# A graph layer's opening: index loads behind the first rows of x, and ACT's order fixed in the tables

## The chip, the cores and the metric

The kernel runs on one core of one Trainium2 chip. The metric is device time in microseconds (us) of one execution, lower being better. The engines are named as in the profile: PE (matrix products and transposes), PEld (PE's weight loads), DVE (vector), ACT (scalar), POOL (GpSimd) and SP (which here only issues DMAs).

## The reference

One layer of a graph network on 6,250 nodes with 128 features and 100,000 edges, sorted by destination, followed by a residual and a layer norm:

```python
msg_in = concatenate([x[src], x[dst]], axis=-1)
h = relu(msg_in @ Wm1 + bm1)
h = relu(h @ Wm2 + bm2)
messages = h @ Wm3 + bm3
agg = segment_sum(messages, dst) / clip(count(dst), 1)
upd = relu(concatenate([x, agg], axis=-1) @ Wn1 + bn1) @ Wn2 + bn2
out = layernorm(x + (x + upd))
```

All data are float32, the indices int32.

## The kernel before

**Three stages.** The product with `Wm1` is taken per node and not per edge: A = x @ Wm1[:128] and B = x @ Wm1[128:] are written to two tables in DRAM, `atab` (float32) and `btab` (each row as three bfloat16 terms whose sum is the float32 row). The main loop then takes the edges in 196 groups of 512, in four pieces of 128: it gathers rows of A by `src` (POOL's indirect DMA, L412), loads a window of rows of B for each piece (SP, L418), spreads them by one-hot matrices made from the destinations, and runs the second product, and sums by destination into `acc` in SBUF. A last stage updates the nodes. The change lies in the tables, but for one copy that it puts into the main loop.

**Loads at the start.** SP loads x into `x_sb` (first tiles 0 and 1, then 2 and 3, then block 1, then two blocks at a time; a block is four tiles of 128 nodes), then `w2`, `w3` and `wu1`. ACT loads `w1` and then `dst_i`, the destinations; POOL loads `src_i`, the sources, and five bias vectors. From `dst_i`, DVE works out each piece's first node: `dst_f` (L190) and its reductions down to `diag` (L274).

**The tables.** There are 13 blocks of nodes (`BLOCKS`; the last has one tile). Round i of the loop at L336 stands in PE's list, which is the order written here since PE is under a manual schedule:

- `turn(4 * i + 4)`: the next block's four transposes into a bank of `pp` (3 buffers), which ACT copies to `xT` (L267). Block 0 is turned ahead of the loop.
- `a_table` for tiles 4i and 4i + 2: `products` of two tiles into a bank of `pb` (5 buffers), copied by ACT (L241) into one of 6 buffers of `brow`, and written by SP to `atab` (L242).
- at i = 6 `starts()`: three products against `diag` whose results (`spread`) DVE copies out (L283 to L296); at i = 7 and 8 `columns`, which transposes the indices into `srcT` and `dloc` (L304, L306).
- `b_table` for tiles 4(i - 3) and on: ACT casts the product (first term, L249), DVE takes the rest (L250, after which the bank is free), POOL casts the rest (second term, L252; ACT at L254 for the last four blocks), DVE takes the third term (L255), SP writes the row to `btab` (L256).
- from i = 12 on, `x_part` for blocks 0 to 2 (`X_BESIDE`): two products of a whole block with `wu1` (L316), each taken out with the bias by ACT (L318) or DVE (L320). Blocks 3 to 8 (`X_BEHIND`) follow the loop.

After the loop `destinations` is called three times: a one-element copy by DVE (L357) that makes the load wait for `srcT`, and two DMAs on ACT's queue of destinations, spread over partitions (`db`, L361). From there to group 6 of the main loop ACT and DVE too are under a manual schedule. POOL clears `acc` in 24 pieces (L376). `pb3` (L381) is a small product whose result DVE adds (L382).

**Order.** Outside the manual schedules a scheduler sets each engine's order from priorities and its own estimates, so a line's place in the source isn't its place in the engine's list; `tc.high_priority()` puts the first loads ahead. Each engine works through its list in order, and a wait holds what stands behind it.

**The copy of the destinations.** `dpad` is a copy of `dst` in DRAM with filler at its end, read only by a loop at L611 that handles windows too wide for one pass and does not run for these inputs. Its two DMAs (L539, L540) stand in the source at group 16 of the main loop; the scheduler had put the first of them behind `wu1`'s load, at 14 us.

Of the kernel before, what the change touches and what calls it, by code (L numbers as in the profile page):

```python
# [11 lines left out]
I32 = mybir.dt.int32  # L12
# [3 lines left out]
ENG = mybir.EngineType  # L16
# [3 lines left out]
P = 128  # L20
# [7 lines left out]
def kernel(  # L28
# [122 lines left out]
    with tc.tile_pool(name="prep", bufs=1) as prep, tc.tile_pool(  # L151
# [8 lines left out]
        nc.vector.memset(dst_i[tail:, :], NONE)  # L160
        with tc.high_priority():
            nc.scalar.dma_start(w1, wm1.rearrange("(k p) h -> p k h", p=P))
            load_rows(nc.scalar, dst_i, dst)
            load_rows(nc.gpsimd, src_i, src)
            with nc.allow_non_contiguous_dma(reason="a bias, one value a partition"):
                nc.gpsimd.dma_start(b1, bm1.rearrange("(c p) -> p c", p=P))
                nc.gpsimd.dma_start(b2, bm2.rearrange("(c p) -> p c", p=P))
                nc.gpsimd.dma_start(b3, bm3.rearrange("(c p) -> p c", p=P))
                nc.gpsimd.dma_start(bu1, bn1.rearrange("(c p) -> p c", p=P))
            nc.gpsimd.dma_start(nb2[:, 0, :], bm2.rearrange("(o h) -> o h", o=1).to_broadcast([P, H]))  # L170

            xb = x[:NTF * P, :].rearrange("(b p i) d -> p b i d", p=P, i=4)
            for i0 in (0, 2):
                nc.sync.dma_start(x_sb[:, i0:i0 + 2, :], xb[:, 0, i0:i0 + 2])
            t = 4
            for n in (4, 8, 8, 8, 8, 8):
                n = min(n, NTF - t)
                nc.sync.dma_start(x_sb[:, t:t + n, :].rearrange("p (b i) d -> p b i d", i=4),
                                  xb[:, t // 4:(t + n) // 4])
                t += n  # L180
            assert t == NTF
            nc.sync.dma_start(x_sb[:N - NTF * P, NTF, :], x[NTF * P:, :])
        nc.sync.dma_start(w2, wm2.rearrange("(k p) h -> p k h", p=P))
        nc.sync.dma_start(w3, wm3.rearrange("(k p) h -> p k h", p=P))
        nc.sync.dma_start(wu1, wn1.rearrange("(k p) h -> p k h", p=P))
# [31 lines left out]

        order = ExitStack()
        order.enter_context(tc.manual_schedule(engines={ENG.PE}))

# [15 lines left out]
        def a_table(t0):  # L236
            m = min(2, NT - t0)
            pbt = products(t0, m, 0)
            bt = brow.tile([P, 2 * 3 * H], BF16, name="bt")
            rows = bt[:, :2 * 2 * H].bitcast(F32).rearrange("p (t h) -> p t h", t=2)  # L240
            nc.scalar.copy(rows[:, :m], pbt[:, :m])  # L241
            nc.sync.dma_start(atab[t0 * P:(t0 + m) * P, :].rearrange("(t p) h -> p t h", p=P), rows[:, :m])  # L242

        def b_table(t0):
            m = min(2, NT - t0)
            pbt = products(t0, m, 1)
            bt = brow.tile([P, 2 * 3 * H], BF16, name="bt").rearrange("p (t c h) -> p t c h", t=2, c=3)
            rest = brow.tile([P, 2, H], F32, name="rest", bufs=2)
            nc.scalar.copy(bt[:, :m, 0], pbt[:, :m])  # L249
            nc.vector.tensor_sub(rest[:, :m], pbt[:, :m], bt[:, :m, 0])  # L250
            if t0 < 4 * LATE:
                nc.gpsimd.tensor_copy(bt[:, :m, 1], rest[:, :m])  # L252
            else:
                nc.scalar.copy(bt[:, :m, 1], rest[:, :m])  # L254
            nc.vector.tensor_sub(bt[:, :m, 2], rest[:, :m], bt[:, :m, 1])  # L255
            nc.sync.dma_start(btab[t0 * P:(t0 + m) * P].rearrange("(t p) c h -> p t c h", p=P), bt[:, :m])  # L256

        def turn(t0):
            m = min(4, NT - t0)
            pt = pp.tile([P, 4, P], F32, name="pt", tag="pp")  # L260
            for i in range(m):
                n = min(P, N - (t0 + i) * P)
                nc.tensor.transpose(pt[:, i, :n], x_sb[:n, t0 + i, :], ident[:n, :n])
            w = min(m * P, N - t0 * P)
            block = xT[:, t0 * P:t0 * P + w]
            if m == 4:
                nc.scalar.copy(block.rearrange("p (n i) -> p i n", i=4), pt)  # L267
            else:
                nc.scalar.copy(block, pt[:, 0, :w])
# [53 lines left out]
        def whole(steps):  # L323
            for _ in steps:
                pass
# [9 lines left out]
        turn(0)  # L335
        for i in range(BLOCKS + BEHIND):  # L336
            if i + 1 < BLOCKS:
                turn(4 * i + 4)
            if i < BLOCKS:
                for t0 in range(4 * i, min(4 * i + 4, NT), 2):  # L340
                    a_table(t0)
            if i == INDICES:
                starts()
            if i - INDICES in (1, 2):
                columns(i - INDICES - 1)
            if i >= BEHIND:
                for t0 in range(4 * (i - BEHIND), min(4 * (i - BEHIND) + 4, NT), 2):
                    b_table(t0)
            if BLOCKS - 1 <= i < BLOCKS - 1 + len(X_BESIDE):
                whole(x_part(X_BESIDE[i - BLOCKS + 1], bank_pb, (nc.scalar, nc.scalar)))  # L350

        def destinations(g, ng, dst_row):

            db = ld.tile([P, 2, 2 * P], I32, name="db", bufs=3)
# [7 lines left out]
            return [db[:, k, :] for k in range(ng)]  # L362

        dst_row = dst.rearrange("(o e) -> o e", o=1)
        early = [destinations(2 * k, 2, dst_row) for k in range(3)]

        turns = ExitStack()
        turns.enter_context(tc.manual_schedule(engines={ENG.DVE, ENG.Activation}))
        for b in X_BEHIND:
            whole(x_part(b, bank_pb, (nc.scalar, nc.vector)))  # L370

# [23 lines left out]
    with edge, tc.tile_pool(name="wk", bufs=2) as wk, tc.tile_pool(  # L395
# [136 lines left out]
        for i in range(NG + ahead + 1):  # L532
            if i == 6:
                turns.close()
            if i == 16:
                late_loads()
                none = wk.tile([16, (NG * GE - E) // 16], I32, name="none", bufs=1)
                nc.vector.memset(none, NONE)
                nc.sync.dma_start(dpad[:E].rearrange("(p e) -> p e", p=16), dst.rearrange("(p e) -> p e", p=16))  # L539
                nc.sync.dma_start(dpad[E:].rearrange("(p e) -> p e", p=16), none)  # L540
            for step, after in enumerate((20, 24, 27)):
                if i >= after and (i - after) % 8 == 0 and (i - after) // 8 < len(pieces):
                    double((i - after) // 8, step)
# [252 lines left out]
```

## Time and profile before

| | |
|---|---|
| median of 5 runs | 1449.77 us (1447.51 to 1451.92) |
| the profiled execution | 1450.33 us, span 1448.6 us |
| mean granted clock of PE | 0.987 |
| busy share of the span | PE 86%, PEld 63%, DVE 46%, ACT 31%, POOL 56% |
| bytes read and written in DRAM | 168.92 MB and 22.88 MB, 132 GB/s over the span |
| first transposes, first product of the tables | 3.86 us, 9.81 us |
| first gather, last line of `btab` issued | 66.79 us, 78.5 us |
| first product of the main loop | 90.77 us |

In a line of a timeline the columns are the start in us, the time in us from there to the end of the last of the merged instructions, the engine, the line of the kernel, the operation with its output and inputs, shapes, and the number of instructions; in brackets stands how long the engine was idle before it and what ended that. An engine with a "q" is its queue, where a DMA is issued. In a table by stages each stretch has busy us and instructions of PE, PEld, DVE, ACT and POOL, then the granted clock of PE (1.00 is full), the mean busy share of the 16 DMA engines, and GB/s.

### The profile page before, as it was taken

The numbers are of one execution on the slowest core, as the hardware profiler recorded it, in microseconds if no ns is written. First come the engines' busy times: TensorE is split into PE (matmuls) and PEld (weight loads), VectorE is DVE, ScalarE is ACT, GpSimd is POOL, SyncE is SP. The second block draws the span as 40 slices with busy tenths as digits, with TensorE's granted clock in tenths as the row PEclk, the third lists the DMA queues.
The fourth block names the chain that finished last, engine by engine and source line by source line (L and its number), as shares of the span: only waits on it lengthen the run. The fifth ranks groups of instructions, "written<-read, shape, count | busy, mean of one in ns | idle before, by whom it ended". The sixth has DMA issues, their size and how long they took to land. (4 is left out here: it accounts for less than half of the span.)

```text
span 1448.6 us, 32804 instructions
## 1 busy us (share of the span) xinstructions
PE 1249.0 (86%) x11196; PEld 918.3 (63%) x11197; DVE 661.1 (46%) x2083; ACT 453.1 (31%) x1160; POOL 805.7 (56%) x859
## 2 busy tenths in 40 slices
PE   7978888888888888888888888898888888888997
PEld 6746666666666666666666666666666666666656
DVE  5733444444443434444444444444443444434487
ACT  5632323232322323232222323232232322323246
POOL 7356565555656556555556556555555556555031
PEclk9989999999999999999999999999999999999999
DMA  8855565555444444444444444444444444443043
GB/s 277 301 154 145 147 162 143 159 139 149 125 122 124 117 128 122 124 114 124 125 121 127 116 127 125 121 114 124 125 124 127 116 125 126 123 122 108 14 146 113
DMA packets 173672, 193.66 MB, mean 134 GB/s; under 512 B 30844, under 2 KB 145486, under 8 KB 173488
## 3 DMA queue, kind: packets, MB, share of 16 engines
q0 software_dynamic: 37984, 103.35, 26.4%
q1 hardware_dynamic: 106956, 61.93, 14.5%
q10 hardware_dynamic: 28564, 26.27, 6.6%
q8 instruction: 90, 1.47, 0.4%
q14 instruction: 78, 0.64, 0.1%
HBM read 168.92 MB, written 22.88 MB: 132 GB/s over the span
## 5 line engine op out<-in xcount | busy, mean ns | idle before, releaser
L412 POOL DMA_INDIRECT ag<-atab,srcT x784 | 753.6, 961 | 524.4 <-PE ph L455 310.6
L469 PE MATMUL ph<-w,h 128*128 128x256 f32 x3128 | 736.5, 389 | 1.4 <-issue 1.4
L469 PEld LDWEIGHTS ph<-w,h 128*128 128x128 f32 x3128 | 583.7, 192 | 158.7 <-issue 61.9
L460 ACT ACTIVATE h<-ph,b 128x256 f32<-128x256 f32 x782 | 306.3, 474 | 914.1 <-PE ph L455 824.5
L471 DVE TENSOR_TENSOR h<-ph,nb 128x512 f32<-128x512 f32 x391 | 269.7, 692 | 688.6 <-PE ph L449 294.1
L455 PE MATMUL ph<-oht,bw 64*128 64x128 bf16 x1564 | 126.8, 217 | 159.8 <-issue 151.2
L455 PEld LDWEIGHTS <-bw 64*128 64x128 bf16 x1564 | 67.4, 95 | 201.4 <-issue 174.3
L494 DVE TENSOR_TENSOR acc<-acc,pt 128x63 f32 x782 | 172.9, 221 | 30.6 <-PE pt L489 2.3
L449 PE MATMUL ph<-ident,ag 64*128 64x64 f32 x3128 | 133.0, 223 | 13.6 <-DVE b L382 7.4
L478 PE MATMUL pg<-h,oh 128*32 128x257 f32 x1564 | 129.8, 397 | 3.2 <-PE ph L455 2.3
L449 PEld LDWEIGHTS ph<-ident,ag 64*128 64x128 f32 x3128 | 114.3, 139 | 13.2 <-DVE b L382 7.5
L433 DVE TENSOR_SCALAR oht<-db,pbase 128x128 bf16<-128x128 int32 x392 | 104.3, 296 | 5.5 <-remote 5.1
L489 PEld LDWEIGHTS pt<-ident,part 64*128 64x128 f32 x1173 | 51.0, 136 | 65.6 <-issue 64.5
L481 ACT COPY part<-pg 128x257 f32<-128x257 f32 x196 | 76.6, 391 | 4.0 <-PE pg L478 4.0
L489 PE MATMUL pt<-ident,part 64*128 64x64 f32 x1173 | 77.7, 238 | 0.0
L436 DVE TENSOR_TENSOR oh<-iota_n,dloc 128x128 f32<-128x128 f32 x196 | 55.7, 284 | 2.8 <-PE pg L478 1.9
L677 POOL TENSOR_TENSOR agg<-total,rc 128x512 f32<-128x512 f32 (+2 forms) x15 | 16.0, 1069 | 70.1 <-DVE total L674 63.3
L232 PE MATMUL pbt<-w,xT 128*128 128x256 f32 x196 | 49.0, 396 | 2.0 <-ACT bt L241 1.4
L478 PEld LDWEIGHTS pg<-h,oh 128*32 128x32 f32 x1564 | 32.1, 108 | 27.2 <-issue 6.1
L232 PEld LDWEIGHTS pbt<-w,xT 128*128 128x128 f32 x196 | 37.0, 198 | 10.5 <-ACT bt L241 2.6
L252 POOL CAST bt<-rest 128x512 bf16<-128x512 f32 x18 | 12.2, 686 | 26.9 <-DVE rest L250 17.9
L700 PEld LDWEIGHTS pot<-wu,u 128*128 128x128 f32 (+1 forms) x196 | 24.0, 191 | 5.1 <-issue 4.5
(110 smaller groups left out, 418.9 us busy)
## 6 DMA issues: line engine op xcount, KB each, us to landing
bw<-btab SPq DMA_DIRECT2D x782, 32.0 KB
db<-in_dst_dram ACTq DMA_DIRECT2D x194, 128.0 KB
ag<-atab,srcT POOLq DMA_INDIRECT x784
btab<-bt SPq DMA_DIRECT2D x24, 384.0 KB
atab<-bt SPq DMA_DIRECT2D x24, 256.0 KB
xd<-in_x_dram SPq DMA_DIRECT2D x12, 256.0 KB
x2tab<-xd SPq DMA_DIRECT2D x12, 256.0 KB
x_sb<-in_x_dram SPq DMA_DIRECT2D x5, 512.0 KB
```

What stands on the lines that cost most here:

```text
L232: nc.tensor.matmul(pbt[:, a, :], xT[:, (t0 + a) * P:(t0 + a + 1) * P], w1[:, k, :], start=True, stop=True)
L412: nc.gpsimd.indirect_dma_start(out=ag[:, j, :], out_offset=None, in_=atab[:, :], in_offset=bass.IndirectOffsetOnAxis(ap=idx[:, j:j + 1], a ...
L433: nc.vector.tensor_scalar(oht[:n, k, :], db[:n, k * P:(k + 1) * P], pb_cols[:n, k:k + 1], None, op0=ALU.is_equal)
L449: nc.tensor.matmul(phs[h][:, c, u * NQ:(u + 1) * NQ], ag[halves[h], u, c * P:(c + 1) * P], ident[halves[h], halves[h]], is_transpose=True, ...
L455: nc.tensor.matmul(phs[h][:, c, k * P:(k + 1) * P], bw[halves[h], k, c * P:(c + 1) * P], oht[halves[h], k, :], start=False, stop=True, ski ...
L460: nc.scalar.activation(h1[:, c, h * 2 * P:(h + 1) * 2 * P], phs[h][:, c, :], AF.Relu, bias=b1[:, c:c + 1])
L469: nc.tensor.matmul(ph2[:, a, :], h1[:, c, (j0 + a) * P:(j0 + a + 1) * P], w2[:, c, :], start=(c == 0), stop=(c == HC - 1))
L471: nc.vector.tensor_tensor(h2[:, j0:j0 + 2, :H], ph2, nb2.to_broadcast([P, 2, H]), op=ALU.max)
L478: nc.tensor.matmul(pg[j * WN:(j + 1) * WN, :], oh[:, j, :], h2[:, j, :], start=True, stop=True, skip_group_check=True)
L481: nc.scalar.copy(part[:n, :], pg[:n, :])
L489: nc.tensor.matmul(pt[:, c, :], rows, ident[halves[h], halves[h]], is_transpose=True, start=True, stop=True, skip_group_check=True)
L494: nc.vector.tensor_add(window, window, pts[j // 2][:, :, k:k + WB])
```

## The change

- `dst_i` and `src_i` are loaded from POOL's queue, without high priority, as are the biases; ACT's queue starts with `w1` alone.
- In round 0 the first `a_table` stands ahead of the second block's transposes; the other rounds are as before.
- The last four blocks' b rows get their later terms (`b_terms`) one table later.
- `destinations` is called in rounds 10, 11 and 12, behind the b tables, and not after the loop.
- The x parts of blocks 0 to 2 are taken out by ACT and DVE, and not by ACT alone.
- ACT is under a manual schedule from the start of the tables: its order is that of the source.
- `dpad` gets its filler first, over an end that is 16 elements longer, so that the copy of `dst` has to wait for it and stays at group 16.

```diff
         with tc.high_priority():
             nc.scalar.dma_start(w1, wm1.rearrange("(k p) h -> p k h", p=P))
-            load_rows(nc.scalar, dst_i, dst)
-            load_rows(nc.gpsimd, src_i, src)
...
...
             nc.sync.dma_start(x_sb[:N - NTF * P, NTF, :], x[NTF * P:, :])
+
+        load_rows(nc.gpsimd, dst_i, dst)
+        load_rows(nc.gpsimd, src_i, src)
...
...
         order.enter_context(tc.manual_schedule(engines={ENG.PE}))
+        turns = ExitStack()
+        turns.enter_context(tc.manual_schedule(engines={ENG.Activation}))
...
+        unfinished = []
         def b_table(t0):
...
             nc.vector.tensor_sub(rest[:, :m], pbt[:, :m], bt[:, :m, 0])
+            unfinished.append((t0, m, bt, rest))
+            if len(unfinished) > 1 or t0 < 4 * LATE:
+                b_terms()
+
+        def b_terms():
+            t0, m, bt, rest = unfinished.pop(0)
             if t0 < 4 * LATE:
                 nc.gpsimd.tensor_copy(bt[:, :m, 1], rest[:, :m])
...
+        early = []
         turn(0)
         for i in range(BLOCKS + BEHIND):
-            if i + 1 < BLOCKS:
-                turn(4 * i + 4)
-            if i < BLOCKS:
-                for t0 in range(4 * i, min(4 * i + 4, NT), 2):
-                    a_table(t0)
+            tiles = range(4 * i, min(4 * i + 4, NT), 2) if i < BLOCKS else []
+            for n, t0 in enumerate(tiles):
+                if n == (i == 0) and i + 1 < BLOCKS:
+                    turn(4 * i + 4)
+                a_table(t0)
...
+            if BLOCKS - 3 <= i < BLOCKS:
+                early.append(destinations(2 * len(early), 2, dst_row))
             if BLOCKS - 1 <= i < BLOCKS - 1 + len(X_BESIDE):
-                whole(x_part(X_BESIDE[i - BLOCKS + 1], bank_pb, (nc.scalar, nc.scalar)))
+                whole(x_part(X_BESIDE[i - BLOCKS + 1], bank_pb, (nc.scalar, nc.vector)))
+        b_terms()
-        early = [destinations(2 * k, 2, dst_row) for k in range(3)]
-        turns = ExitStack()
-        turns.enter_context(tc.manual_schedule(engines={ENG.DVE, ENG.Activation}))
+        turns.enter_context(tc.manual_schedule(engines={ENG.DVE}))
...
             if i == 16:
                 late_loads()
-                none = wk.tile([16, (NG * GE - E) // 16], I32, name="none", bufs=1)
+                none = wk.tile([16, (NG * GE - E) // 16 + 1], I32, name="none", bufs=1)
                 nc.vector.memset(none, NONE)
+                nc.sync.dma_start(dpad[E - 16:].rearrange("(p e) -> p e", p=16), none)
                 nc.sync.dma_start(dpad[:E].rearrange("(p e) -> p e", p=16), dst.rearrange("(p e) -> p e", p=16))
-                nc.sync.dma_start(dpad[E:].rearrange("(p e) -> p e", p=16), none)
```

By the built programs, POOL's 24 memsets of `acc`, which stood almost all ahead of its first cast, now stand as 6 ahead of the first cast, 1 behind it, 4 behind the second, and 5 and 8 behind the next two pairs; and DVE's share of an early x part stands ahead of the rests of the two b tables written before it.

More of the change, by code (lines that the diff above doesn't have):

```diff
@@ L162 @@
             nc.scalar.dma_start(w1, wm1.rearrange("(k p) h -> p k h", p=P))
-            load_rows(nc.scalar, dst_i, dst)
-            load_rows(nc.gpsimd, src_i, src)
[L165 to L170, printed above, removed]
             xb = x[:NTF * P, :].rearrange("(b p i) d -> p b i d", p=P, i=4)
@@ L182 @@
             nc.sync.dma_start(x_sb[:N - NTF * P, NTF, :], x[NTF * P:, :])
+        load_rows(nc.gpsimd, dst_i, dst)
+        load_rows(nc.gpsimd, src_i, src)
+        with nc.allow_non_contiguous_dma(reason="a bias, one value a partition"):
+            nc.gpsimd.dma_start(b1, bm1.rearrange("(c p) -> p c", p=P))
+            nc.gpsimd.dma_start(b2, bm2.rearrange("(c p) -> p c", p=P))
+            nc.gpsimd.dma_start(b3, bm3.rearrange("(c p) -> p c", p=P))
+            nc.gpsimd.dma_start(bu1, bn1.rearrange("(c p) -> p c", p=P))
+        nc.gpsimd.dma_start(nb2[:, 0, :], bm2.rearrange("(o h) -> o h", o=1).to_broadcast([P, H]))
         nc.sync.dma_start(w2, wm2.rearrange("(k p) h -> p k h", p=P))
@@ L333 @@
         assert sorted(X_BESIDE + X_BEHIND + X_FIRST + X_END) == list(range(BLOCKS))
-        turn(0)
-        for i in range(BLOCKS + BEHIND):
-            if i + 1 < BLOCKS:
-                turn(4 * i + 4)
-            if i < BLOCKS:
-                for t0 in range(4 * i, min(4 * i + 4, NT), 2):
-                    a_table(t0)
[L342 to L349, printed above, removed]
-                whole(x_part(X_BESIDE[i - BLOCKS + 1], bank_pb, (nc.scalar, nc.scalar)))
         def destinations(g, ng, dst_row):
@@ L364 @@
         dst_row = dst.rearrange("(o e) -> o e", o=1)
-        early = [destinations(2 * k, 2, dst_row) for k in range(3)]
-        turns = ExitStack()
-        turns.enter_context(tc.manual_schedule(engines={ENG.DVE, ENG.Activation}))
+        early = []
+        turn(0)
+        for i in range(BLOCKS + BEHIND):
+            tiles = range(4 * i, min(4 * i + 4, NT), 2) if i < BLOCKS else []
[3 more added lines that the diff above has]
+                a_table(t0)
+            if i == INDICES:
+                starts()
+            if i - INDICES in (1, 2):
+                columns(i - INDICES - 1)
+            if i >= BEHIND:
+                for t0 in range(4 * (i - BEHIND), min(4 * (i - BEHIND) + 4, NT), 2):
+                    b_table(t0)
+            if BLOCKS - 3 <= i < BLOCKS:
+                early.append(destinations(2 * len(early), 2, dst_row))
+            if BLOCKS - 1 <= i < BLOCKS - 1 + len(X_BESIDE):
+                whole(x_part(X_BESIDE[i - BLOCKS + 1], bank_pb, (nc.scalar, nc.vector)))
+        b_terms()
+        turns.enter_context(tc.manual_schedule(engines={ENG.DVE}))
         for b in X_BEHIND:
```

## The prediction

> **What bounds the kernel now.** I read the busy time by stages first, to see where the edited code runs and what is full there; then the timelines of PE, ACT, DVE, POOL and SP up to 95 us, because every edit but one lies before the first group of edges. The main loop, from 91 us on, executes the same groups after the change as before, so the question is when it starts.
>
> Stages (us of the stretch, busy us of each engine, clock, DMA share):
>
> ```profile
> 14.00:24.00 10.00, 9.78 (x50) 8.22 (x48) 7.10 (x17) 6.38 (x10) 9.02 (x13) 1.00 1.03 359
> 36.00:50.00 14.00, 13.47 (x79) 11.61 (x78) 13.79 (x29) 8.50 (x14) 3.31 (x5) 1.00 0.76 264
> 50.00:63.00 13.00, 11.67 (x51) 8.40 (x49) 8.02 (x13) 8.45 (x16) 4.14 (x7) 1.00 0.98 344
> 63.00:83.00 20.00, 19.67 (x57) 10.43 (x57) 13.41 (x21) 14.14 (x26) 13.76 (x15) 1.00 0.85 283
> 83.00:91.00 8.00, 0.58 (x9) 0.50 (x9) 1.87 (x10) 0.69 (x1) 3.42 (x4) 0.73 0.33 98
> ```
>
> The first number after the stretch is PE's. PE carries the tables (90 to 98% busy from 14 to 83 us), DVE is as full from 36 to 50, DMA is full at 14 to 24 and 50 to 63, and from 83 to 91 everything is idle.
>
> PE's timeline at the two ends of the tables:
>
> ```profile
> 8.90 1.11 PE L263 MATMUL pt<-ident,x_sb 128*128 128x128 f32 x4 [2.02 <-DMA x_sb<-in_x_dram]
> 9.81 3.62 PE L232 MATMUL pbt<-w,xT 128*128 128x256 f32 x8
> 14.07 2.34 PE L232 MATMUL pbt<-w,xT 128*128 128x256 f32 x8
> ...
> 36.72 0.60 PE L263 MATMUL pt<-ident,x_sb 128*128 128x128 f32 x4
> ...
> 60.52 2.42 PE L232 MATMUL pbt<-w,xT 128*128 128x256 f32 x10 [0.55 <-ACT bt L241]
> 72.47 10.55 PE L316 MATMUL pxu<-xT,wu 128*128 128x512 f32 x24
> 90.77 1.12 PE L449 MATMUL ph<-ident,ag 64*128 64x64 f32 x16 [7.42 <-DVE b L382]
> ```
>
> I write a0, a2, ... and b0, b2, ... for the products of `a_table` and `b_table`. a0 starts at 9.81, behind the second block's transposes, which wait for x; a4 starts at 14.07; b38, the last b ahead of the x parts, ends at 62.94; the last x part ends at 83.02; the first group starts at 90.77.
>
> POOL, ACT, and SP's loads of the first groups:
>
> ```profile
> 7.23 15.79 POOL L376 MEMSET acc<- 128x784 f32 x21
> 66.79 1.05 POOL L412 DMA_INDIRECT ag<-atab,srcT  x1 [2.58 <-DMA atab<-bt]
> 46.71 1.42 ACTq L361 DMA_DIRECT2D db<-in_dst_dram  x2
> 48.24 1.07 ACT L249 CAST bt<-pbt 128x512 bf16<-128x512 f32 x2 [3.93 <-PE pbt L232]
> 64.78 14.07 SPq L256 DMA_DIRECT2D btab<-bt  x9
> 82.81 33.65 SPq L418 DMA_DIRECT2D bw<-btab  x32
> ```
>
> The chain that opens the main loop is the last line of `btab`: issued at 78.51, landed at 81.94, first `bw` issued at 82.81, the fourth at 89.83, first L455 at 91.67. Beside it runs the x parts' chain: L320 at 89.90, L382 at 90.57, which frees the bank for L449. Both end within 2 us of each other, so a gain must move both.
>
> **The change part by part.**
>
> *First rows.* Without `dst_i` on ACT's queue and `src_i` on POOL's at 1.3 us, x's first three pieces and `w1` (0.77 MB) are alone. At 0.3 MB a us (0.24 up to 14 us, 0.36 from there to 24), from the first packet at 2.7 us, and with the 0.7 us from bytes to landing, block 1 is there at about 6, not 8.86. The first transposes then end at about 4.9, ACT's copy (1.07) at 6.0, a0 takes 1.8 (half of the 3.62, at that same rate), the moved transposes 1.1, a2 1.8 and the next transposes about 0.7: a4 at about 11.1 instead of 14.07. **Lead 3.0**; 3.4 with the faster clock that in this trace comes 5 us after a0.
>
> *Indices.* `dst_i` now follows POOL's iotas (about 2.6 us instead of 1.29) and is POOL's DMA. `src_i` by that queue took 7.3 us from issue to landing, `dst_i` by ACT's 5.4. So `dst_f` starts at about 10.5 (before 10.24), and `diag`, which ended at 21.46, is needed at 33.3. Cost 0; cover 12 us. The Trainium skill, "SBUF — State Buffer", in its warning on DVE blocking a POOL DMA, speaks against the move: POOL cannot write descriptors while DVE holds the shared port, and its example grows from 0.6 to 3.1 us. Here POOL's three `src_i` issues took 0.75, 0.53 and 0.49 beside DVE's two 0.91 memsets, so the trace does not show it; by the rule the three issues of `dst_i` would be 7.5 us later, still inside that cover, and the sum the same.
>
> *`dpad` held back.* Its 390 KB sat between the weights and the first `atab` row in SP's queue: a0 landed at 21.34, 0.64 behind it, while `dpad` took 0.95. a12's copy reuses a0's buffer, so it moves from 23.81 to about 20.5 (in the old order it also stood behind a block copy). At group 16 the copy costs SP one issue (0.83) and the queue 0.95, with `bw` loaded up to four groups, some 25 us, ahead. Cost 0 there, 2 at worst.
>
> *POOL's order.* This gives most of the lead back. The memsets used to run in one piece to 23.0; now POOL's list is 6 memsets, cast, 1, cast, 4, two casts, 5, two casts, 8, two casts. It starts later (ten DMA issues ahead, to about 9.6), does 6 by 14, and waits for b0's rest at about 23. Then five memsets and two casts are 5 x 0.70 + 1.2 = 4.7 us, eight and two 6.8, where a block of PE takes 4.3. DVE's third term waits for each cast, and behind it stand the copies of `spread` that free PE's banks. By hand: b4's cast 28.0, b8's 33.0, first copy of `spread` 34.9 (35.87 before), next transposes 35.4 (36.72 before), `dloc` 42.9 (43.36 before). **Lead 3.5 falls to 0.6** at 44 us. If POOL's waits cost nothing the 3.5 stays; if memsets slow to the longest, 1.29, three more us are lost.
>
> *ACT's order.* The `db` loads waited for DVE with ACT's copies behind them (3.93 us, the line at 48.24); they now stand at the last three blocks. That stall let DMA run idle and then full, and PE lost time at 50 to 63: b20 to b38 needs 15.2 us at PE's rate and took 18.0. I take all 2.8 as recovered: **lead 3.3, b38 at 59.6**. Bounds 0 and 2.8, as the six `db` loads, some 2.5 us of DMA, still fall there.
>
> *x parts and late terms.* Half of each early x part goes to DVE, and in DVE's list it stands ahead of the `rest` that frees the next b's bank. A round (two x products, two b products) is 3.44 on PE; the chain is now x product 0.86, 0.28 to DVE, L320 0.70, rest 0.65, term 0.60, rest 0.65, x product 0.86 = 4.6. Three rounds cost 3.5, less a stall of 0.39 that goes: **+3.2 for the last x product**. The last `btab` line is hurt less, since before it stood behind two x copies on ACT: by the same steps 17.2 behind b38 instead of 15.6, **+1.6**.
>
> *Sum.* Last `btab` issue: -3.3 + 1.6 = -1.7, at 76.8. It landed 3.4 after issue in a full queue; a lone line took 2.5 (42.16 to 44.65), which I take as -0.8. `bw` then starts 2.5 earlier; the first gather, behind `atab`'s last row, about 2.2 earlier. The x parts end where they did (-3.3 + 3.2), but their last copies at 84.1, 87.7 and 89.9 were not PE-paced: PE had issued at 83. The trace names "issue" and "remote" for that wait, no cause; SP's four loads also took 7.0 us where the next four took 2.4, while the first sixteen gathers ran (to 87.34). I let both end with the gathers, 2.2 to 2.5 earlier; bounds 0 and 7.
>
> Profiled execution 1450.33 - 2.5 = 1447.8; it lies 0.56 above the median of the runs, so **1447.3**. Anything within 0.2% (2.9 us) a measurement can hardly tell from no change.
>
> **The rivals.**
>
> *The gap closes.* If the wait from 83 to 90.8 came from how the last x copies and the gathers fell together, it need not come back: `bw` in 2.4 us instead of 7.0 gives 4.6 more, 1442 to 1443. For it: the loads after it ran at 0.65 each. Against: nothing in the change removes the gathers beside it. The trace drops the clock to 0.50 at 86.66, 3.6 us after PE's last product, until 96.9. The Trainium skill, "TensorE: Matmul & The Clock Gate", part 1, has the clock halve after an idle window of about 3.4 us; by it a shorter gap would also save half of the 6.1 us from 90.77 to 96.9, so 1439.5, a figure no row here shows.
>
> *Nothing is left.* x is no earlier, since the queue is full to 24 us either way, or the lead is all given back: 1449 to 1451.
>
> *Slower.* DVE's list decides at the x parts. If b38 ends after 61.5 (the stalls at 50 to 63 stay, as DMA was at 0.98), the last x product ends at 84.7 or later, and if the 7.4 us follow it, the start is 2 to 4 us later: 1452 to 1454. It decides if the wait is tied to PE's last product, not to the gathers.
>
> **How the numbers follow.** Forecast 45%, own range 1445 to 1449.5: 0.18 of it below 1446.9, 0.27 within. Gap closes 25%, faster. Nothing left 10%, same. Slower 20%. So 0.43, 0.37, 0.20. The range 1441 to 1453 leaves out the cold-clock saving below and the end of the slower case.
>
> **What would show it.** Right: a4 at about 11, POOL's memsets still running at 39, next transposes after `spread` near 35.4, no ACT wait ahead of the `db` loads, PE waits of about 1 us among the early x parts, first `bw` near 80.3, first group near 88. Wrong: POOL's memsets done by 30 (then the lead is 3 more), x parts gapless on PE, or a first group before 85 or after 91.

## The result, and the profile after

The changed kernel takes 1449.70 us (median of 26 runs, 1446.49 to 1455.03), the kernel before, run beside it, 1450.17 (47 runs): ratio 0.9996, 95% interval 0.9989 to 1.0004. No difference can be measured. The profiled execution took 1450.53 us, span 1448.8 (before 1450.33 and 1448.6). The forecast was 1447.3, range 1441 to 1453.

The experiments ran on several chips, on which the kernel before took 1209, 1429 and 1450 us. Each is compared with the kernel before on its own chip, and traces are set side by side only where the text says from which chips.

The stages after, columns as in the prediction's table of before (the last stretch reaches past the first product of the main loop, now at 88.17):

```profile
14.00:24.00 10.00, 8.60 (x46) 7.32 (x45) 5.50 (x12) 5.34 (x8) 2.83 (x5) 1.00 0.97 323
36.00:50.00 14.00, 10.74 (x45) 8.34 (x44) 13.70 (x23) 5.75 (x9) 7.08 (x11) 0.76 0.49 174
50.00:63.00 13.00, 13.00 (x71) 11.48 (x70) 9.55 (x17) 8.43 (x15) 4.59 (x6) 1.00 0.83 287
63.00:83.00 20.00, 19.22 (x60) 10.36 (x59) 15.73 (x25) 13.54 (x27) 9.62 (x11) 1.00 0.92 309
83.00:91.00 8.00, 5.28 (x31) 2.79 (x29) 3.86 (x16) 1.82 (x3) 6.17 (x7) 0.99 0.51 160
```

PE is full from 50 to 63, as forecast, where it had lost 1.3 us. But it lost 1.2 us more at 14 to 24 and 2.7 more at 36 to 50, where its clock fell to 0.76 as well. PE's timeline shows where:

```profile
6.50 2.08 PE L235 MATMUL pbt<-w,xT 128*128 128x256 f32 x4 [1.14 <-ACT xT L279]
12.10 1.98 PE L235 MATMUL pbt<-w,xT 128*128 128x256 f32 x8
22.84 3.13 PE L235 MATMUL pbt<-w,xT 128*128 128x256 f32 x12 [1.40 <-ACT bt L244]
36.84 0.66 PE L275 MATMUL pt<-ident,x_sb 128*128 128x128 f32 x4 [0.44 <-DVE base L295]
43.61 2.08 PE L235 MATMUL pbt<-w,xT 128*128 128x256 f32 x4 [2.82 <-DVE groups_i L308]
46.33 3.61 PE L235 MATMUL pbt<-w,xT 128*128 128x256 f32 x8
49.75 0.28 PE L314 MATMUL pd<-ident,dst_f 98*128 98x98 f32 x1
60.09 5.79 PE L235 MATMUL pbt<-w,xT 128*128 128x256 f32 x26
76.33 10.69 PE L328 MATMUL pxu<-xT,wu 128*128 128x512 f32 x24 [0.41 <-DVE xT L332]
88.17 0.72 PE L464 MATMUL ph<-ident,ag 64*128 64x64 f32 x16 [0.81 <-DVE xT L332]
93.81 0.29 PE L470 MATMUL ph<-oht,bw 64*128 64x128 bf16 x2 [4.72 <-issue]
96.51 0.50 PE L470 MATMUL ph<-oht,bw 64*128 64x128 bf16 x5 [2.41 <-DMA btab<-bt]
100.51 3.87 PE L484 MATMUL ph<-w,h 128*128 128x256 f32 x16
```

a4 starts at 12.10 instead of 14.07, the next transposes after `spread` at 36.84 instead of 36.72: the lead is gone. The second `columns` start at 49.75 (before 43.48). From there to the x parts 3.3 us are won back: b38 ends 2.9 behind (65.88 against 62.94). The last x product ends at 87.02 (83.02), the second products of group 0 (L484) start at 100.51 (95.94). The lines of before for three of these:

```profile
37.69 0.55 DVE L287 CAST tilei<-base 1x784 int32<-1x784 f32 x1
...
43.48 0.25 PE L302 MATMUL pd<-ident,dst_f 98*128 98x98 f32 x1
...
95.94 4.17 PE L469 MATMUL ph<-w,h 128*128 128x256 f32 x16
```

ACT's wait at 22, DVE and POOL at 36 to 41, and the two queues that open the main loop:

```profile
22.20 1.23 ACT L244 COPY bt<-pbt 128x512 f32<-128x512 f32 x2 [4.32 <-DMA atab<-bt]
...
37.45 3.67 DVE L299 CAST tilei<-base 1x784 int32<-1x784 f32 x1
...
35.10 5.59 POOL L391 MEMSET acc<- 128x784 f32 x8
...
73.02 1.56 POOL L427 DMA_INDIRECT ag<-atab,srcT  x1 [5.63 <-DMA db<-in_dst_dram]
...
86.33 13.51 SPq L433 DMA_DIRECT2D bw<-btab  x8
```

`tilei`'s cast, 0.55 us before, took 3.67 and ended at 41.12, 0.43 behind the last of eight memsets on POOL (35.10 + 5.59 = 40.69). DVE's `rest` operations, which free b's banks, stand behind the cast: the first ran from 42.89 to 43.56, and PE, which had waited 2.82, started at 43.61. The first gather comes at 73.02 (66.79), and SP needs from 86.33 to 96.72 for the four `bw` loads of group 0 (before 82.81 to 89.83).

So the main loop opens 4.6 us later, and yet the total is the same. The starts of the first gathers of groups 12 and 195, read from POOL's timeline in both traces, before and then after:

```profile
146.80 0.95 POOL L412 DMA_INDIRECT ag<-atab,srcT  x1 [1.77 <-PE ph L455]
1337.45 0.96 POOL L412 DMA_INDIRECT ag<-atab,srcT  x1 [1.62 <-PE ph L455]
```

```profile
151.20 0.95 POOL L427 DMA_INDIRECT ag<-atab,srcT  x1 [1.90 <-PE ph L470]
1337.62 0.95 POOL L427 DMA_INDIRECT ag<-atab,srcT  x1 [1.71 <-PE ph L470]
```

That stretch of the loop, called L below, takes 1190.7 us before and 1186.4 after; what follows it takes 111.1 and 111.2. The tables lost 4.4 us and the loop won 4.2. Two questions, then: what took the time in the tables, and why does the same loop run faster?

### The profile page after: what moved, and what is told of

Its sections match the earlier page's. It is cut to its first block, busy times and chain, and to the rows that moved or that the text cites. A ratio compares the mean times of both kernels' runs of the same rounds, so it can differ in the third digit from the quotient of the medians.

```text
span 1448.8 us, 32816 instructions
## 1 busy us (share of the span) xinstructions
PE 1246.8 (86%) x11196; PEld 917.5 (63%) x11197; DVE 662.9 (46%) x2086; ACT 451.9 (31%) x1157; POOL 803.3 (55%) x862
## 3 DMA queue, kind: packets, MB, share of 16 engines
q1 hardware_dynamic: 106956, 61.93, 14.6%
## 5 line engine op out<-in xcount | busy, mean ns | idle before, releaser
L484 PE MATMUL ph<-w,h 128*128 128x256 f32 x3128 | 731.9, 387 | 0.0
L484 PEld LDWEIGHTS ph<-w,h 128*128 128x128 f32 x3128 | 581.5, 191 | 153.8 <-issue 59.0
L470 PE MATMUL ph<-oht,bw 64*128 64x128 bf16 x1564 | 126.5, 217 | 173.7 <-issue 153.8
L470 PEld LDWEIGHTS <-bw 64*128 64x128 bf16 x1564 | 67.6, 94 | 215.2 <-issue 185.1
```

Of the source, the lines that this page charges most:

```text
L470: nc.tensor.matmul(phs[h][:, c, k * P:(k + 1) * P], bw[halves[h], k, c * P:(c + 1) * P], oht[halves[h], k, :], start=False, stop=True, ski ...
L484: nc.tensor.matmul(ph2[:, a, :], h1[:, c, (j0 + a) * P:(j0 + a + 1) * P], w2[:, c, :], start=(c == 0), stop=(c == HC - 1))
```

## The experiments

My theory (A) was that ACT's order gains about 3 us and that POOL's memsets beside `tilei` lose them again; the rivals were (B) that the opening is set by the first gathers and `bw` loads, so that the tables don't count, and (C) that `tilei`'s cast is slow for its own form. A further theory (G) was that the gathers slow SP.

**e1: the memsets first** (chip of 1209 us).

```diff
+        # behind the index and bias loads, ahead of the tables
+        for c in range(HC + 1):
+            for k in range(8):
+                nc.gpsimd.memset(acc[:, c, k * PIECE:(k + 1) * PIECE], 0.0)
```

> The changed kernel with POOL's 24 memsets of acc ahead of all its casts, behind the index and bias loads. Theory A (POOL's order cost the lead): in the changed kernel eight memsets lay beside DVE's cast of tilei (L299), which took 3.67 us instead of 0.55, and b products waited 2.82 for it. Then here the cast takes 0.5 to 0.9, the first column transposes start near 44 to 46 instead of 49.75, the first gather comes near 68 instead of 73.0, the main loop starts 3 to 5 us earlier than in the changed kernel, and the time is 1445 to 1447. Theory B (the start is set elsewhere, by the loads of bw beside the first gathers): the cast is short again but the first L470s end where they did within 1.5 us, or the time stays at 1449 to 1450.5. Theory C (tilei's cast is slow for its own form, not for the memsets): it takes 3 us or more here too.

Ratio 1.0003 (0.9994 to 1.0012). POOL, DVE and PE in its trace:

```profile
11.96 16.70 POOL L187 MEMSET acc<- 128x784 f32 x24
...
14.10 14.58 DVE L204 TENSOR_SCALAR lm<-lm 98x8 f32<-98x8 f32 x1
...
32.45 2.07 PE L239 MATMUL pbt<-w,xT 128*128 128x256 f32 x4 [8.40 <-DVE rest L259]
```

`tilei`'s cast was 0.55 us, but the stall had moved: an operation of 98x8 elements waited 14.6 us, to 28.68, two hundredths behind the end of POOL's row (28.66). So it is not one cast that is slow beside memsets: here, too, DVE stood until a row of memsets ended, this time 21 of them. In h1 below the same operation took 6.87, to 21.13, with a row of twelve that ended at 21.11; but it took 0.49 beside 21 memsets in the kernel before and 0.16 to 0.71 in the other traces, so it doesn't happen each time. This profiled execution was the longest of its 12 runs (1215.09, median 1208.77), so the others, which were not traced, need not have had a stall of this size. A and B were not told apart; C fell.

**e2: the front only** (1209). The kernel before, with the index loads moved and the first rows ahead:

```diff
-            load_rows(nc.scalar, dst_i, dst)
-            load_rows(nc.gpsimd, src_i, src)
...
+        load_rows(nc.gpsimd, dst_i, dst)
+        load_rows(nc.gpsimd, src_i, src)
...
+                if n == (i == 0) and i + 1 < BLOCKS:
+                    turn(4 * i + 4)
+                a_table(t0)
```

> The kernel before with two parts of the change only: the index loads on POOL's queue behind the first of x, and the first rows of A ahead of the second block's transposes; ACT's order, the destinations, the x parts and dpad as before. By the trace of the changed kernel the first rows are worth 2.0 us at a4 (12.1 instead of 14.07). POOL's list here has 15 memsets ahead of the first cast and 3, 1, 3, 1, 1 between casts. Theory A (the memsets between casts give the lead back): a4 near 12, but the first columns no earlier than before (43 to 47), the time 1449 to 1452. Rival (the lead lasts, since only three memsets in a row are left): columns near 41.5, the time 1447.5 to 1448.5.

Ratio 0.9998 (0.9987 to 1.0010). a4 started at 11.65 and the second columns at 41.25: the lead held to there, as the rival had it, but the time did not follow. 0.9 us ahead of e3 there, it starts the x parts 1.5 behind it (61.12 and 59.59): between lie five waits of 0.29 to 0.55 for ACT and DVE, where e3 has one of 0.50. The front alone gains nothing that the time shows.

**e3: ACT's order only** (1209). The changed kernel with the loads, the first rows and `dpad` of before; what stays of the change:

```diff
+        turns.enter_context(tc.manual_schedule(engines={ENG.Activation}))
...
+            if BLOCKS - 3 <= i < BLOCKS:
+                early.append(destinations(2 * len(early), 2, dst_row))
...
+                whole(x_part(X_BESIDE[i - BLOCKS + 1], bank_pb, (nc.scalar, nc.vector)))
+        b_terms()
```

> The changed kernel with its front taken back: index loads, first rows and dpad as in the kernel before; ACT's order from the source, the destinations in rounds 10 to 12, the late terms and the x parts over two engines stay. POOL's list is that of before (21 memsets first). If the order of ACT is worth what the changed kernel's trace shows (2.6 us between turn 36 and b38, less 1.1 more in the x parts), b38 ends near 60.2 instead of 62.94, the last x product near 81.5, and the time is 1448 to 1449. If the opening of the main loop is set by bw loads beside the gathers, b38 is as early but the first L470s end near 92 as before and the time is 1449.5 to 1450.5. If it makes ACT wait elsewhere (its copies of atab stood 4.3 us in the changed kernel), the time is 1450.5 to 1452.

Ratio 0.9972 (0.9961 to 0.9982), faster by 3.4 us by the ratio (medians 1205.15 and 1208.81). PE's waits from 50 to 60 are one of 0.50. Of the parts that were run alone this is the one that gains. Where all of the 3.4 us are won the traces don't show: the kernel before has none on this chip, and against e2, whose time is that of before, e3's PE is 1.8 us ahead at group 2 (93.8 and 95.6), 1.0 at group 12, and 2.3 only from group 36 on, behind waits of e2 for `acc` that e3 does not have.

**e4: gathers held** (1209). POOL was to read group 0's `bw` ahead of group 1's gathers:

```diff
+                if i == 1:
+                    probe = wk.tile([P, 2, 1], F32, name="probe", bufs=1)
+                    nc.gpsimd.tensor_copy(probe, st[0]["got"][1][:, :, :1])
```

> The changed kernel, but POOL waits for group 0's bw before it issues the gathers of group 1, so that 4 and not up to 12 gathers lie beside the first bw loads. In the changed kernel's trace SP's instructions took about 0.7 us each from 85.6 to 96.7, the time in which the first sixteen gathers ran, and 0.03 to 0.47 after it. Theory G (the gathers slow SP): the four bw loads of group 0 take 2.4 to 3 us instead of 10, the second and third L470 of group 0 come at 89 to 91 instead of 93.8 and 96.5, and, since gathers (1.26 us each) keep up with 6.5 us a group, the time is 2 to 5 us lower, 1445 to 1448. Theory H (SP is slow there for another reason, or the profile makes it slow): bw loads take 7 us or more as before, and the time is the same or up to 6 us higher, as the gathers of groups 1 to 3 come later.

The edit did not do what it was meant to: POOL's order is the scheduler's there, and the reading stood behind the seventeenth gather (at 92.91). It says nothing on G. But it is in effect the changed kernel on this chip: ratio 1.0010 (0.9999 to 1.0022), `tilei`'s cast 3.67 again, PE's wait 2.83, no drop of the clock there, the second columns at 45.42 where e3 has 42.17. POOL's gathers then run 2.0 to 4.0 us behind e3's to the last group (median 3.6). On this chip the start is carried through to the total.

**f0 and f1: both kernels again** (1450).

> The kernel before, unchanged, for its trace on the chip of these runs, where it took 1208.8 us and not 1450. If that chip only does without the issue waits of the main loop (0.86 us a group ahead of L455 and those of its weight loads), the tables look as in the first trace (first columns at 43.5, b38's end near 63, the last x product near 83), SP's loads of bw take 0.65 each, and the opening of the main loop lies near 85.

> The changed kernel, unchanged. Theory A (ACT's order gains 3.4 us, as e3 showed, and the memsets beside tilei lose it): as in e4, tilei's cast takes over 3 us, PE waits 2.8 us for groups_i, the last x product ends near 84.7, the ratio to before is 0.999 to 1.001. Rival (e4's wait of POOL, and not the change, cost e4 its time): the ratio is 0.996 to 0.998.

f0: 1449.95, the opening as in the first trace (second products of group 0 at 95.04), L 1191.0; its expectation, written for the other chip, says nothing here. f1: ratio 0.9994 (0.9985 to 1.0002), theory A's band, but with L's help: its gathers of group 12 start 3.65 behind f0's (146.04). PE, DVE and POOL in f1's timeline:

```profile
10.67 1.89 PE L235 MATMUL pbt<-w,xT 128*128 128x256 f32 x8
...
35.91 3.67 DVE L299 CAST tilei<-base 1x784 int32<-1x784 f32 x1
...
42.09 1.13 PE L235 MATMUL pbt<-w,xT 128*128 128x256 f32 x4 [2.83 <-DVE groups_i L308]
...
149.69 0.95 POOL L427 DMA_INDIRECT ag<-atab,srcT  x1 [1.63 <-PE ph L470]
```

The cast's 3.67 comes to the hundredth in all three traces with this list on POOL. a4 starts at 10.67, 3.3 ahead of f0's 13.97, and the transposes after `spread` at 35.31, still 1.2 ahead (36.54). The clock at 43 did not fall this time. So the second columns were 2.1 behind f0's (45.35 and 43.30) and not 6.3; L is 1185.9.

**f2: POOL by hand** (1450). The changed kernel with POOL's order written out:

```diff
+        turns.enter_context(tc.manual_schedule(engines={ENG.Pool}))
...
+        clear(12)          # 12 of the 24 memsets, ahead of the rounds
...
+            if 9 <= i < 12:
+                clear(4)   # behind the round's casts
```

> The changed kernel with POOL under the manual schedule of the tables too: 12 memsets ahead of the first cast, none until round 9, then four behind the casts of each of the rounds 9 to 11, when tilei, the starts and the columns are done. Theory A: tilei's cast takes 0.55, the wait of 2.8 for groups_i is gone, the second columns start near 41.5 to 42 instead of 45.4, the main loop starts 3 to 3.5 us earlier than in f1, and the ratio to before is 0.9965 to 0.998. Rival (the loss comes from the front: the index loads or the first rows): no more than 1 us earlier than f1, ratio 0.999 to 1.001.

Ratio 0.9973 (0.9960 to 0.9986), 3.9 us by the ratio; against f1, on the same chip, 1446.21 and 1449.29. DVE, POOL and PE in its timeline:

```profile
34.94 0.55 DVE L309 CAST tilei<-base 1x784 int32<-1x784 f32 x1
...
67.27 1.55 POOL L436 DMA_INDIRECT ag<-atab,srcT  x1 [3.35 <-issue]
...
93.34 1.22 PE L493 MATMUL ph<-w,h 128*128 128x256 f32 x2
...
145.90 0.95 POOL L436 DMA_INDIRECT ag<-atab,srcT  x1 [1.86 <-PE ph L479]
```

The cast is short, PE waits for nothing from 36 to 50, the first gather comes 4.0 earlier than f1's (71.27), the second products of group 0 6.35 earlier (99.69), group 12's gathers 3.8 earlier (145.90 against 149.69), and L is 1186.7, near f1's. So the loss of theory A is shown: with the memsets elsewhere the long cast, PE's wait and 3.8 us at group 12 are gone. Its gain is not shown on this chip: f2's last x product ends 1.5 us earlier than f0's (81.24 and 82.69), but the first gather comes 0.8 later and group 12's gathers are level (145.90 and 146.04), so that f2's gain over the kernel before lies in L.

**f3: the old index loads** (1450). The changed kernel, but for:

```diff
-        load_rows(nc.gpsimd, dst_i, dst)
-        load_rows(nc.gpsimd, src_i, src)
...
+            load_rows(nc.scalar, dst_i, dst)
+            load_rows(nc.gpsimd, src_i, src)
```

> The changed kernel with the index loads back on ACT's and POOL's queues at the start; first rows of A ahead, dpad held back, ACT's order kept. POOL's list is then 15 memsets, two casts, 5, two casts, 4 and the other casts, so that the last memsets end ahead of tilei. If the index loads matter only through POOL's order, tilei's cast takes 0.55 to 0.9 and the ratio is that of e3 or a little lower, 0.9965 to 0.998. If moving them is worth time by itself, since the first of x lands earlier, a4 is back near 13 and the ratio is 0.998 to 0.9995. If the first rows gain nothing behind the full DMA queue, the spread products start near 30.5 here as in e3 and e4.

A miss: ratio 1.0018 (1.0005 to 1.0031), slower than any of its alternatives allowed, though the cast took 0.55, a4 started at 12.82 and the second columns at 42.61. Group 12's gathers start 2.3 us later than f0's (148.38 and 146.04), and L is 1191.5, as in the kernel before, where the changed kernel has 1186. The loop's lists are the same as the changed kernel's, in both traces. PE's timeline has it done with the x parts at 83 and waiting:

```profile
92.33 1.12 PE L465 MATMUL ph<-ident,ag 64*128 64x64 f32 x16 [9.27 <-DVE b L398]
```

The first gather came at 68.48, 2.0 later than f0's 66.46: in SP's list `atab`'s last row now stands behind two more lines of `btab`. The opening followed that, not PE.

**g1 to g3**, on the chip of 1429 us. g1 is f2 with e4's edit, which POOL's written order now holds:

> f2 (POOL by hand) with e4's edit: POOL waits for group 0's bw before it gathers for group 1. e4 ran on the chip where the kernel before takes 1209 us and SP's loads are quick in any case (0.65 each), so it could not show what gathers do to them; in f2 on the chip of 1450 us the four loads of group 0 were issued from 79.2 to 89.4, and the gathers ran from 67.3. Theory G (the gathers slow SP's instructions): on the chip of 1450 us the fourth load is issued by 82.5, the second products of group 0 (L484) start 2.5 us or more before f2's 93.3, groups 1 to 3 are not late, and the ratio to before is 0.9945 to 0.997. Theory H (SP is slow at that time whatever POOL does): the fourth load is issued at 88 or later and the ratio is 0.997 to 1.001. On the chip of 1209 us no difference from f2, 0.996 to 0.998.

SP, POOL and PE in its timeline:

```profile
80.05 4.25 SPq L442 DMA_DIRECT2D bw<-btab  x6
...
84.35 0.20 POOL L578 CAST probe<-bw 128x2 f32<-128x2 bf16 x1 [10.32 <-PE ph L473]
...
88.10 3.72 PE L493 MATMUL ph<-w,h 128*128 128x256 f32 x16 [1.56 <-ACT x_sb L340]
...
109.48 1.48 PE L473 MATMUL ph<-ident,ag 64*128 64x64 f32 x16 [13.70 <-ACT h L484]
```

G's first half is shown: with POOL held from 74 to 85, the four loads went out from 80.05 to 82.16, and the second products of group 0 started 6.0 earlier than g3's (94.14). Its second half failed: the burst came later, from 85 to 105, and then it was ACT that stood (from 89.5 to 108.2) and PE that waited 13.7 for it. Ratio 1.0018 (1.0009 to 1.0028), by the medians 6.8 us worse than g3. The burst's cost is moved, not saved.

g2 is f2 with eight loads of 512 bytes that nothing uses:

```diff
+            for k in range(3):
+                nc.scalar.dma_start(x2tab[k:k + 1, :], x[k:k + 1, :])
...
+        for k in range(3, 8):
+            nc.gpsimd.dma_start(x2tab[k:k + 1, :], x[k:k + 1, :])
```

> f2 with eight loads of 512 bytes more at the start, three on ACT's queue and five on POOL's, that nothing uses (into rows of x2tab that are written again later), which shifts the count of DMAs on either side of the main loop's by as much (modulo 8) as leaving the index loads where the kernel before has them. On the chip of 1450 us the main loop from the gathers of group 12 to those of group 195 took 1190.7 and 1191.0 in the kernel before and 1191.5 in f3, but 1186.4, 1185.9 and 1186.7 in the changed kernel (twice) and f2, with the loop's lists in f3 as in the changed kernel. Theory P (the loop's pace depends on the phase in which its DMAs meet the semaphores that they take in turn): the loop takes 1190 to 1192 here, the ratio to before is 0.9995 to 1.002. Rival (it doesn't): 1186 to 1187 and the ratio of f2, 0.996 to 0.998. On the chip of 1209 us the loop takes 962 to 965 either way.

L is 1170.6, where g1 and g3 on this chip have 1165.2 and 1166.1; the ratio is 0.9999 (0.9986 to 1.0011), and f2's gain is gone, though group 12's gathers start as in g3 (146.48 and 146.66). So the count of small loads ahead of the loop, by queue, moves the loop's pace by 4.5 to 5.4 us, as much as the index loads' move did. The test is not quite clean, since DVE's and SP's lists in the loop differ from g3's at some places up to 535 us; but 3.1 of the 4.5 us arise behind that, from group 80 on, and f3 has no such difference. Each is one trace, and the lag inside the loop is not steady (g2 is level with g3 at group 48 and 1.6 behind at group 60). That it is the semaphores' phase is my guess at the mechanism; the runs show the dependence alone.

g3 is f2 with `atab`'s last row on ACT's queue:

```diff
-            nc.sync.dma_start(atab[...], rows[:, :m])
+            (nc.scalar if t0 + 2 >= NT else nc.sync).dma_start(atab[...], rows[:, :m])
```

> f2 with atab's last row written from ACT's queue behind its copy, and not from SP's, where it stands behind two rows of btab. In f2 the first gather came at 67.3. If it is held by that row alone, it comes at 65 to 66; if the gathers slow SP's loads of bw, these then come free of them 1 to 2 us earlier, and the ratio to before is 0.996 to 0.9975. If the first gather waits for POOL's own list (its last memsets end near 66), or the loads of bw are slow anyway, nothing moves: 0.997 to 0.9985.

First gather at 65.05, ratio 0.9965 (0.9954 to 0.9977), the lowest of all on its chip, but f2's interval covers it; `bw`'s loads were no freer than g2's (82.25 to 88.08, and 79.24 to 85.38).

**h1: three buffers** (a chip of 1208 us). g3 with:

```diff
-            ag = ld.tile([P, GT, H], F32, name="ag", bufs=4)
+            ag = ld.tile([P, GT, H], F32, name="ag", bufs=3)
```

> g3 with three buffers for the gathered rows (ag) and not four: the first burst has 12 gathers and not 16, and every list of instructions is that of g3. By g1, SP's four loads for group 0 take 2.1 us when no gathers stand beside them, and a burst slows whatever engine issues then (in g1 it was ACT, 13.7 us). Theory G (the burst as such is the cost): here the burst ends near 81 and not 86, the fourth bw load of group 0 is issued by 85 (g3: 88.1), the second products of group 0 start near 89 to 91 (g3: 94.1), the gathers of group 3 follow once group 0 has been read and are no longer in the way, and the ratio to before is 0.992 to 0.9955. Rival (three buffers are too few for the main loop, where a group's gathers take 5.0 of its 6.4 us): the loop from group 12 to 195 is 5 us or more longer than g3's and the ratio is 0.998 or higher. Rival (what is won at group 0 is lost at groups 1 to 3, as in g1): the gathers of group 12 start no earlier than g3's 146.7 and the ratio is 0.9955 to 0.9975. On the chip of 1209 us: 0.996 to 0.998 by any of them but the first rival.

Ratio 0.9967 (0.9955 to 0.9978), 1204.43 against 1208.15; L 964.5, as e4's 964.1, so three buffers are enough there. Its own question, the shorter burst's worth where bursts slow the other engines, could not be answered on this chip and stays open. What it adds is that f2's idea gains on such a chip too.

Together (us; "columns" is the start of the second `columns`, "group 0" that of its second products, L as above):

| kernel | chip | ratio | columns | first gather | group 0 | L |
|---|---|---|---|---|---|---|
| before, f0 | 1450 | 1 | 43.5, 43.3 | 66.8, 66.5 | 95.9, 95.0 | 1190.7, 1191.0 |
| changed, f1 | 1450 | 0.9996, 0.9994 | 49.8, 45.4 | 73.0, 71.3 | 100.5, 99.7 | 1186.4, 1185.9 |
| f2 | 1450 | 0.9973 | 42.4 | 67.3 | 93.3 | 1186.7 |
| f3 | 1450 | 1.0018 | 42.6 | 68.5 | 97.4 | 1191.5 |
| g1 | 1429 | 1.0018 | 42.7 | 68.8 | 88.1 | 1165.2 |
| g2 | 1429 | 0.9999 | 42.1 | 66.1 | 94.2 | 1170.6 |
| g3 | 1429 | 0.9965 | 42.1 | 65.0 | 94.1 | 1166.1 |
| e1 | 1209 | 1.0003 | 52.1 | 75.6 | 98.3 | 964.0 |
| e2 | 1209 | 0.9998 | 41.3 | 64.7 | 89.1 | 964.6 |
| e3 | 1209 | 0.9972 | 42.2 | 68.0 | 88.0 | 962.5 |
| e4 | 1209 | 1.0010 | 45.4 | 71.4 | 91.1 | 964.1 |
| h1 | 1208 | 0.9967 | 42.3 | 66.2 | 87.8 | 964.5 |

Theory A holds for its loss; its gain is seen only in the totals of e3 and h1, on the chips of 1209 and 1208 us. B holds in so far as on the chips of 1450 and 1429 us the gathers set the opening; but the tables set the first gather, so they count.

## Why the prediction was right and wrong

The range held the time, the likeliest case did not: a start 2.5 us earlier was forecast, and it came 4.6 later, hidden by a faster loop. That the time lies in the range is luck: a loss and a gain of some 4 us, neither of which the sum had, cancelled. The rival "nothing is left" gave the right time, by half of its reason. The gap did not close: group 0's four `bw` loads spread over 10.4 us instead of 7.0. The rule that the prediction cites from the Trainium skill, "TensorE: Matmul & The Clock Gate", part 1, and the estimate of 1439.5 by it, were not put to the test: PE's clock was at half for 10.2 us in both traces, from 86.7 before and from 90.8 after. By the steps:

- **First rows, near:** the lead at a4 was 2.0 in the first pair of traces and 3.3 in f1 against f0, where 3.0 to 3.4 was forecast (the terms given for a4's start add up to 11.4, not 11.1). Block 1 landed at 8.59 and, in f1, at 7.62, not at 6; but PE came to its transposes at 8.63 and 8.29 without a wait. In f1 the products of a2 took 1.26 us, in the first trace 1.91.
- **`dpad`, near in f1:** a0's row was to land at about 20.4 and a12's copy to follow at 20.5. They came at 22.09 and 22.20 in the first trace (21.34 and 23.81 before) and at 20.63 and 20.74 in f1 (21.30 and 23.70 in f0). Ahead of that copy ACT still stood 4.3 us, and PE lost 1.4 behind it instead of 0.7.
- **Indices, right:** `dst_f` at 11.50 and, in f1, 11.05 (10.5 forecast), `diag` done at 19.74 and 19.05, both covered. The rule on DVE blocking a POOL DMA cost nothing that can be seen.
- **POOL's order, the step that failed.** The sum had 0.6 us of lead left at 44. Up to 36 f1 ran as forecast (the transposes after `spread` at 35.31, 35.4 forecast); then the second columns were 2.1 behind, and 6.3 in the first trace, where the clock fell as well. The bound held three more us, but for memsets that slow down, while what happened is the reverse: they ran at 0.70 and DVE's cast waited for the last five of the row of eight. I priced each of POOL's pieces by hand and never asked which DVE operation falls beside them. f2 shows the term: 3.8 us at group 12 against f1.
- **ACT's order, right in kind.** 2.8 forecast; from the second columns to b38 3.3 regained in the first pair of traces, 1.6 in f1 and 2.5 in f2 against f0; and 3.4 us of the total in e3, with the `db` loads, late terms and x parts that go with it.
- **x parts, mis-sized:** from b38's end to the last x product it took 1.1 us more than before in the first pair (21.1 and 20.1), 2.4 in f1 and 1.9 in f2 against f0, not 3.2; in the first trace the waits are 0.36 and 0.41, not a longer round. It did not matter here, as PE's last product does not set the opening.
- **First gather, wrong sign:** 2.2 earlier was forecast, it came 6.2 later, and 4.8 in f1. The memsets are most of it (f2's comes 4.0 before f1's); f3 shows another 2.0 that I did not look for, SP's list, in which `atab`'s last row moved back.
- **"Both end with the gathers", right.** In the six traces from chips of 1450 us the fourth `bw` load goes out 1.3 to 2.8 us after the sixteenth gather ends (89.83 after 87.33, 96.72 after 94.14), and the second products of group 0 start 26.1 to 29.2 after the first gather. In g2 it goes out 1.1 ahead of that end (85.38 and 86.47), so the tie is not exact. g1 shows that the gathers are the cause. The prediction's "everything is idle" from 83 to 91 misread its own row: POOL was busy for 3.42 of the 8 us.
- **The premise that the loop is the same in both kernels, wrong.** L is 1190.7 and 1191.0 before, 1186.4 and 1185.9 after. f3, whose lists in the loop are those of f1, and g2 tie it to the loads ahead of the loop. Why, stays open. Inside L the clock was at half for 17.1 us in both traces of the kernel before, 10.2 in g2 and 3.4 in f3, against 3.4 in the changed kernel and none in f1, f2, g1 and g3; whether that is a cause or follows from the same waits isn't shown, and f3's 3.4 us, which cost PE 1.7 at most, are too few for its L. Without the shorter L the change would have been some 4 us slower (4.4 and 3.65 at group 12), the slower rival's price by another mechanism, which e4 hints at on a chip where L varies less (962.5 to 964.6 in e1 to e4).

The Trainium skill, "SBUF — State Buffer", section "Who interferes with whom", bears on the failed step: a cast or `tensor_scalar` on DVE can take the ports that it shares with GpSimd, whoever issues first has them for the whole instruction, and the other blocks. The traces agree on the block (0.55 alone, 3.67 beside memsets); but it outlasted five memsets and, in e1, 21, more than one instruction's turn.

## What to carry to other kernels

A scheduler that moves cheap fillers (memsets) between an engine's real work can put them beside a small operation of another engine that everything waits for; write the fillers' places down, away from DVE's casts and `tensor_scalar`s. When a part of a change gains and the whole does not, run the parts alone: here ACT's order, with what goes with it, was worth 3.4 us on one chip, and the memsets' new places gave about as much back. And check the stretch that "does not change" against itself in two traces of each kernel before putting a difference of 0.3% down to the edited code.

## What the runs showed of the hardware

The same program took 1209, 1429 and 1450 us on different chips, with equal mean times of PE's instructions in the loop. PE's groups from 150 us to near the loop's end, in the changed kernel on the chip of 1450 us and in e4 on that of 1209 (columns: busy us, mean ns, idle time ahead and its releaser):

```profile
L484 PE MATMUL ph<-w,h 128*128 128x256 f32 x2912 | 678.8, 386 | 0.0
L470 PE MATMUL ph<-oht,bw 64*128 64x128 bf16 x1456 | 118.6, 216 | 161.2 <-issue 144.6 <-DMA db<-in_dst_dram 10.6 <-DMA bw<-btab 4.5
```

```profile
L484 PE MATMUL ph<-w,h 128*128 128x256 f32 x2959 | 688.3, 386 | 0.0
L470 PE MATMUL ph<-oht,bw 64*128 64x128 bf16 x1468 | 71.2, 216 | 0.0
```

On the slower chip PE stands 161 us ahead of L470, mostly with no cause that the trace names; on the faster one not at all. SP's register and DMA instructions differ in the same way: beside the first burst of gathers many of them took 0.7 us or more on the chips of 1450 and 1429 us, while most took 0.03 to 0.5 on that of 1209. What sets the chips apart, and why gathers hold up other engines' instructions on two of them, stays open. So does the clock's rule: it halved at 43.0 in the first trace of the changed kernel, within a wait of 2.82, and not in f1 and e4, with the same wait of 2.83.
